# A written-out order of 1170 words replaced by another: cross-attention on one core, two softmax sums per query

## The chip, the cores and the metric

The kernel runs on one core of one Trainium2 chip. The metric is the time of the program on the device in microseconds (us); less is better. The time given is the median of three runs, and beside it stands one profiled execution, from which every row below comes.

## The reference

Two batches of 2048 tokens with 640 channels attend to 154 context rows with 1024 channels. The first 77 rows are text, the last 77 are an image prompt. There are 20 heads of 32 channels. Each head has two softmaxes, one over the text keys and one over the image keys, and their outputs are added. All is in float32.

```python
q = _split_heads(hidden_states @ Wq.T, H)
k = _split_heads(text @ Wk.T, H)
v = _split_heads(text @ Wv.T, H)
out_text = _merge_heads(_attend(q, k, v, sm_scale))
k_ip = _split_heads(ip @ Wk_ip.T, H)
v_ip = _split_heads(ip @ Wv_ip.T, H)
out_ip = _merge_heads(_attend(q, k_ip, v_ip, sm_scale))
out = (out_text + IP_SCALE * out_ip) @ Wo.T + bo
return out + residual
```

## The kernel before

The work is cut into 20 units. A unit `u` is 1024 tokens by 128 channels (four heads); two units that share batch and channels form the pair `q = u // 2`, and units 0 to 9 are batch 0. A unit has three groups `s` of 3, 3 and 2 tiles of 128 tokens. The scores of a group take four PSUM banks, one for each head, either banks 0 to 3 or banks 4 to 7.

The program is a list of 1170 words, `SCHEDULE`, and `emit` writes out the instructions of one word after another. No loop orders the work: each engine runs its instructions in the order in which the words stand, and waits where an input or a bank is not ready. A planner made the list with prices for instructions and transfers. The words are these; `R1.19@0` is group 1 of unit 19 in banks 0 to 3:

- TensorE (PE): `q` queries of a unit's half; `k`, `v` keys and values; `R` the scores (line L351); `A.q` the weighted sum over the values for a pair (L462), which needs all six groups of the pair transposed; `m`, `n`, `o`, `p`, `F` the output and query products in fast matrix schemes, which take sums of weights and of tokens as operands; `F` are the output products of batch 1, at the end of the list.
- ScalarE (ACT): `K` copies scores from PSUM to the tile `pb` (L363); `E` is the exponential; `CA`, `cq` empty banks.
- VectorE (DVE): `M` the row maxima, `D` the row sums, `I` their reciprocals, `T` the 32x32 transpose (L453), `cm`, `co`, `Y` additions into the output, and those sums of weights, `V....d`, and of tokens, `X....d`, that end in d.
- GpSimd (POOL): `S` subtracts the maxima (L425), `N` multiplies by the reciprocals (L446), and the sums `V....p`, `X....p`, `G`, `t`, `W`.
- SyncE (SP): all transfers but three, in the order of the list.

For a group the chain is R, K, M, S, E, D, I, N, T. Four sets name groups that go another way:

- `DIRECT`: no K and no S. M reads the PSUM banks (L402, four instructions), and E is 24 (or 16) small ScalarE instructions that read the banks with the maximum as bias (L387). The banks are held until E is done.
- `BIASED`: K stays, S goes; E is 24 (or 16) small ones out of `pb`.
- `SUMMED`: of these, E also accumulates the row sums, and D goes.
- `SHIFTED`: no K; VectorE subtracts out of PSUM (L415), and E is one instruction.

Of the kernel before, what the change touches and what calls it, by code (L numbers as in the profile page):

```python
# [9 lines left out]
F32 = mybir.dt.float32  # L10
# [10 lines left out]
def kernel(  # L21
# [43 lines left out]
        (1, 1), (2, 0), (2, 2), (4, 1), (6, 1), (13, 0), (13, 2), (15, 2), (16, 0), (19, 0), (19, 1), (19, 2),  # L65
    }
    BIASED = {
        (1, 2), (3, 2), (4, 2), (5, 2), (6, 2), (7, 0), (8, 0), (9, 2), (10, 0), (10, 2), (11, 2), (12, 0),
        (12, 2), (14, 1), (16, 2), (17, 1), (18, 0),
    }  # L70
    SUMMED = {
        (1, 2), (2, 0), (4, 2), (6, 1), (11, 2), (12, 0), (13, 0), (14, 1), (15, 2), (16, 0), (16, 2), (18, 0),
# [3 lines left out]
        (7, 1), (8, 1), (11, 0), (17, 0),  # L76
# [135 lines left out]
    PLACES = "012340134201342013420130414204102343123404330213"  # L212
    q_places = iter(PLACES)

# [441 lines left out]
    for _ in range(9):  # L656
# [256 lines left out]
    for c, stages in enumerate(chains_of):  # L913
        for _, text in stages:
            for _, t in terms(text):
                for h in range(NH):
                    o = int(t[0]), NH * int(t[1]) + h
# [127 lines left out]
```

## Time and profile before

| | |
|---|---|
| median of 3 runs | 504.8 us (504.4 to 506.38) |
| the profiled execution | 505.93 us, its span 504.1 us |
| mean granted TensorE clock | 0.993 |
| busy: PE, DVE, ACT, POOL | 493.4, 429.0, 335.6, 352.3 us |
| SBUF and DRAM traffic by DMA | 71.51 MB, mean 142 GB/s |

A busy time is the sum of an engine's instructions in the trace. Float32 matmuls show as two records each. A row of the timeline gives the start, the length, the engine, the line and the operation, with "xN" for N instructions merged into one row, and in brackets the idle time of the engine before it and what ended it. The attentions `A.0` to `A.9` started at 68.4, 107.8, 147.06, 184.5, 219.9, 265.8, 309.1, 350.4, 388.34 and 430.9 us, and they serve below as milestones.

### The profile page before, as it was taken

How to read it: one execution, taken by the hardware profiler on the slowest of the kernel's cores; microseconds unless marked ns; L12 is line 12 of the kernel's file. 1: busy time of each engine (PE TensorE's matmuls, PEld its weight loads, DVE VectorE, ACT ScalarE, POOL GpSimd, SP SyncE). 2: the span in 40 equal slices, each digit the busy share in tenths (PEclk: the TensorE clock that was granted, in tenths of full speed). 3: DMA queues.
4: the chain of work that ended last, by engine and by line, in shares of the span. 5: the costliest groups of instructions: out<-in, count | busy, mean ns of one | idle time of the engine just before them, and what ended most of it. 6: DMA issues, size and time to landing. Idle time of an engine off the chain costs nothing.

```text
span 504.1 us, 11093 instructions
## 1 busy us (share of the span) xinstructions
PE 493.4 (98%) x4248; PEld 321.2 (64%) x4248; DVE 429.0 (85%) x473; ACT 335.6 (67%) x1218; POOL 352.3 (70%) x172
## 2 busy tenths in 40 slices
PE   9999999999999999999999999999999989999996
PEld 5756756847645867868687676866755656444443
DVE  0089878997979999999999897999798997898877
ACT  1379988878897786888996987689679584100000
POOL 0087857766877989999898387897448938375730
PEclk9999999999999999999999999999999979999999
DMA  8992260271352526766763654266812001420115
GB/s 294 352 306 67 58 163 2 76 188 32 90 134 100 189 79 200 264 232 207 242 220 111 200 174 148 67 203 217 275 48 84 22 2 62 148 83 1 42 72 220
DMA packets 64996, 71.51 MB, mean 142 GB/s; under 512 B 5552, under 2 KB 46896, under 8 KB 63920
## 3 DMA queue, kind: packets, MB, share of 16 engines
q1 hardware_dynamic: 64256, 70.16, 44.1%
q8 instruction: 33, 0.54, 0.4%
q10 hardware_dynamic: 688, 0.66, 0.4%
q14 instruction: 19, 0.16, 0.1%
HBM read 50.74 MB, written 16.78 MB: 134 GB/s over the span
## 4 chain that ended last, share of the span: by engine, by line
PE 84%; DVE 5%; DMA 4%; ACT 3%; POOL 2%; issue 1%; SPq 1%; DVEq 0%; POOLq 0%
PE bank L218 18%; PE bank L998 11%; PE bank L351 10%; PE bank L462 9%; PE bank L148 9%; PE bank L620 9%; PE bank L302 8%; PE bank L601 5%; ACT pb L387 3%; PE bank L630 2%; PE bank L311 2%; DMA x<-in_x_dram 2%; DVE den L436 1%; DVE pb L977 1%; DMA x<-td 1%
## 5 line engine op out<-in xcount | busy, mean ns | idle before, releaser
L446 POOL TENSOR_TENSOR pb<-pb,rden 128x1848 f32<-128x1848 f32 (+1 forms) x60 | 175.9, 2944 | 51.2 <-DVE rden L441 43.7
L425 POOL TENSOR_TENSOR pb<-pb,mx 128x1848 f32<-128x1848 f32 (+1 forms) x27 | 82.5, 3057 | 52.9 <-DVE mx L399 52.7
L453 DVE STREAM_TRANSPOSE pb<-pb 128x1920 f32<-128x1920 f32 (+1 forms) x60 | 115.1, 1932 | 1.3 <-POOL pb L446 1.0
L399 DVE TENSOR_REDUCE mx<-pb 128x24 f32<-128x1848 f32 (+1 forms) x44 | 80.2, 1824 | 31.5 <-ACT pb L363 31.5
L387 ACT ACTIVATE pb<-pb,mx 128x77 f32<-128x77 f32 x328 | 96.0, 374 | 0.5 <-DVE mx L399 0.3
L436 DVE TENSOR_REDUCE den<-pb 128x24 f32<-128x1848 f32 (+1 forms) x46 | 85.3, 1855 | 9.7 <-ACT pb L387 4.8
L218 PE MATMUL bank<-x,wq_pair 128*128 128x512 f32 x200 | 89.4, 598 | 0.0
L363 ACT COPY pb<-bank 128x462 f32<-128x462 f32 (+1 forms) x176 | 74.3, 531 | 17.0 <-PE bank L351 14.7
L387 ACT ACTIVATE pb<-bank,mx 128x77 f32<-128x77 f32 x256 | 69.7, 398 | 14.9 <-DVE mx L402 14.9
L351 PEld LDWEIGHTS bank<-kT,qT 32*128 32x128 f32 x1280 | 50.7, 186 | 24.4 <-issue 8.5
L351 PE MATMUL bank<-kT,qT 32*128 32x154 f32 x1280 | 62.5, 309 | 3.6 <-ACT pb L387 3.3
L218 PEld LDWEIGHTS bank<-x,wq_pair 128*128 128x128 f32 x200 | 37.7, 192 | 43.4 <-issue 42.7
L462 PE MATMUL bank<-pb,v 32*32 32x512 f32 x1600 | 56.8, 597 | 0.8 <-issue 0.8
L431 ACT ACTIVATE pb<-pb 128x1848 f32<-128x1848 f32 (+1 forms) x31 | 52.1, 1685 | 5.8 <-POOL pb L425 5.7
L148 PE MATMUL bank<-wo_ct,aT 128*128 128x154 f32 x320 | 45.8, 296 | 0.0
L148 PEld LDWEIGHTS bank<-wo_ct,aT 128*128 128x128 f32 x320 | 43.2, 188 | 4.1 <-issue 3.4
L462 PEld LDWEIGHTS bank<-pb,v 32*32 32x32 f32 x1600 | 30.7, 103 | 22.8 <-issue 11.8
L387 ACT ACTIVATION_READ_ACCUMULATOR pb<-bank,mx 128x1 f32 x152 | 40.8, 278 | 0.0
L601 PE MATMUL bank<-aT,wo_ct 128*128 128x512 f32 x80 | 36.3, 596 | 0.0
L402 DVE TENSOR_REDUCE mx<-bank 128x6 f32<-128x462 f32 (+1 forms) x64 | 33.5, 585 | 2.7 <-PE bank L351 2.7
L620 PE MATMUL bank<-aT,wo_ct 128*128 128x256 f32 x128 | 32.0, 384 | 0.0
L387 ACT ACTIVATION_READ_ACCUMULATOR pb<-pb,mx 128x1 f32 x136 | 29.6, 219 | 0.0
(109 smaller groups left out, 657.1 us busy)
## 6 DMA issues: line engine op xcount, KB each, us to landing
x<-in_x_dram SPq DMA_DIRECT2D x12, 1280.0 KB, 7.5
out_dram<-acc SPq DMA_DIRECT2D x19, 256.0 KB, 2.4
acc<-in_x_dram SPq DMA_DIRECT2D x16, 256.0 KB, 3.7
td<-x SPq DMA_DIRECT2D x4, 1024.0 KB, 5.6
x<-td SPq DMA_DIRECT2D x4, 1024.0 KB, 5.6
out_dram<-x SPq DMA_DIRECT2D x15, 256.0 KB, 2.0
v<-vS SPq DMA_DIRECT2D x160, 20.0 KB, 2.1
aT<-in_L_xattn_Wk_ip_dram SPq DMA_DIRECT2D x5, 512.0 KB, 5.2
```

The source lines that it names most:

```text
L148: nc.tensor.matmul(keys_in(out), loaded[n][:, k, :], cT[:, k, :, t, :], start=(k == 0), stop=(k == NCC - 1))
L218: nc.tensor.matmul(pq, wqs[q % 3][:, k, :], xs[place_of(u, h)][:, k, :], start=(k == 0), stop=(k == NC - 1),)
L351: nc.tensor.matmul(ps[g][:, ts(t, 2 * L)], qTs[(u, h)][g * D : (g + 1) * D, ts(st, P)], kT[g * D : (g + 1) * D, c, b].rearrange("p t l -> ...
L363: nc.scalar.copy(keys_of(u, s)[:, :, g], ps[g][:, : n * 2 * L].rearrange("p (n l) -> p n l", n=n))
L387: nc.scalar.activation(row, row if ps is None else rows_in(ps[g], n)[:, t, x], AF.Exp, bias=maxs[(u, s)][:, *one], accum_out=None if den i ...
L399: nc.vector.tensor_reduce(mx, rows_of(u, s), AX.X, ALU.max, negate=negate)
L425: nc.gpsimd.tensor_tensor(rows_of(u, s), rows_of(u, s), maxs[(u, s)].unsqueeze(3).to_broadcast([P, n, 2, L]), ALU.subtract)
L436: nc.vector.tensor_reduce(den_of(u, s), rows_of(u, s), AX.X, ALU.add)
L446: nc.gpsimd.tensor_tensor(rows_of(u, s), rows_of(u, s), rdens[(u, s)].unsqueeze(3).to_broadcast([P, n, 2, L]), ALU.mult)
L453: nc.vector.transpose(p, p)
L462: nc.tensor.matmul(pa[r][g * D : (g + 1) * D, :], v4s[q % 2][rows, g, k, :], zones[rows, :, g, k, :], start=(k == 0), stop=(k == NK - 1),)
L620: nc.tensor.matmul(part, w_of[m][:, kp, op], t_of(m, b, i)[:, kp], start=(op == kp == 0 and m in (1, 2, 5)), stop=(op == 1 and kp == 1 and ...
```

## The change

The list is another one of 1168 words. It holds the same matmuls, the same sums of weights and tokens on the same engines, and the same transfers; what changes is the order, the banks, the buffers of the query tiles (`PLACES`), and the way of eleven groups. Written (unit, group):

| group | before | after |
|---|---|---|
| (0,2) | plain | BIASED |
| (3,1) | plain | DIRECT |
| (6,1) | DIRECT, SUMMED | plain |
| (6,2) | BIASED | plain |
| (7,0) | BIASED | plain |
| (7,2) | plain | BIASED, SUMMED |
| (8,2) | plain | BIASED |
| (9,2) | BIASED | DIRECT |
| (17,0) | SHIFTED | plain |
| (17,1) | BIASED | plain |
| (18,0) | BIASED, SUMMED | plain |
| (18,1) | plain | DIRECT |
| (18,2) | plain | BIASED |

Besides, (10,2) and (12,2) accumulate their sums in E now and (12,0) no longer does. The diff, with two lines of the list:

```diff
     DIRECT = {
-        (1, 1), (2, 0), (2, 2), (4, 1), (6, 1), (13, 0), (13, 2), (15, 2), (16, 0), (19, 0), (19, 1), (19, 2),
+        (1, 1), (2, 0), (2, 2), (3, 1), (4, 1), (9, 2), (13, 0), (13, 2), (15, 2), (16, 0), (18, 1), (19, 0),
+        (19, 1), (19, 2),
     }
     BIASED = {
-        (1, 2), (3, 2), (4, 2), (5, 2), (6, 2), (7, 0), (8, 0), (9, 2), (10, 0), (10, 2), (11, 2), (12, 0),
-        (12, 2), (14, 1), (16, 2), (17, 1), (18, 0),
+        (0, 2), (1, 2), (3, 2), (4, 2), (5, 2), (7, 2), (8, 0), (8, 2), (10, 0), (10, 2), (11, 2), (12, 0),
+        (12, 2), (14, 1), (16, 2), (18, 2),
     }
     SUMMED = {
-        (1, 2), (2, 0), (4, 2), (6, 1), (11, 2), (12, 0), (13, 0), (14, 1), (15, 2), (16, 0), (16, 2), (18, 0),
+        (1, 2), (2, 0), (4, 2), (7, 2), (10, 2), (11, 2), (12, 2), (13, 0), (14, 1), (15, 2), (16, 0), (16, 2),
         (19, 0), (19, 2),
     }
     SHIFTED = {
-        (7, 1), (8, 1), (11, 0), (17, 0),
+        (7, 1), (8, 1), (11, 0),
     }
...
-    PLACES = "012340134201342013420130414204102343123404330213"
+    PLACES = "012340134201432014312032404121024314214303402140"
...
-        "V.D.0.d V.P.1.d V.Q.0.d N1.18 E2.18 CA.8 V.I.0.p X.B.p@2 V.K.0.p V.X.0.p SS.3.4 V.E.0.d R1.19@0 M1.19 E1.19 m5.3@4 "
+        "V.E.0.d SS.3.4 CA.8 I0.18 V.H.0.d I2.18 N2.18 V.T.0.d R1.19@0 m2.3@4 M1.19 cm2.3 V.I.0.p T1.18 m1.3@6 cm1.3 "
```

The first place that matters is VectorE between the row sums of unit 18 and the maxima of group (19,1). In these rows `den_18_1` is written by D1.18 and `rden_18_1` by I1.18; L977 and L975 that write `pb_91` from `wo_ct_98` or `pb_91` are the sums of weights `V`; `mx_19_1` are the maxima M1.19. Before:

```order
L436 TENSOR_REDUCE den_18_1_3722<-pb_91 128x24
L441 RECIPROCAL rden_18_1_3724<-den_18_1_3722 128x24
L977 TENSOR_TENSOR pb_91<-wo_ct_98 128x128 x2
L977 TENSOR_TENSOR pb_91<-pb_91,wo_ct_98 128x128
L975 SCALAR_TENSOR_TENSOR pb_91<-pb_91,wo_ct_98 128x128
L977 TENSOR_TENSOR pb_91<-wo_ct_98 128x128
L402 TENSOR_REDUCE mx_19_1_3841<-bank_0_69 128x3x2
```

And in the changed kernel, from D2.18 on:

```order
L437 TENSOR_REDUCE den_18_2_3806<-pb_91 128x16
L977 TENSOR_TENSOR pb_91<-wo_ct_98 128x128 x2
L977 TENSOR_TENSOR pb_91<-pb_91,wo_ct_98 128x128
L975 SCALAR_TENSOR_TENSOR pb_91<-pb_91,wo_ct_98 128x128
L977 TENSOR_TENSOR pb_91<-wo_ct_98 128x128
L442 RECIPROCAL rden_18_0_3818<-den_18_0_3804 128x24
L977 TENSOR_TENSOR pb_91<-wo_ct_98,pb_91 128x128
L442 RECIPROCAL rden_18_2_3821<-den_18_2_3806 128x16
L977 TENSOR_TENSOR pb_91<-pb_91,wo_ct_98 128x128
L403 TENSOR_REDUCE mx_19_1_3843<-bank_0_69 128x3x2
```

Before, the five sums came behind the reciprocal I1.18, which sets GpSimd going on N1.18; now seven sums come behind D2.18, with two reciprocals among them, and D0.18 and D2.18 stand ahead of them.

The second place is GpSimd between the attentions A.7 and A.8, where `mx` rows (L425, L426 after) are the subtractions S and `rden` rows (L446, L447 after) the multiplications N of the unit and group in the name. Before:

```order
L425 TENSOR_TENSOR pb_91<-pb_91,mx_17_2_3563 128x8x154
L446 TENSOR_TENSOR pb_91<-pb_91,rden_17_1_3600 128x12x154
L446 TENSOR_TENSOR pb_91<-pb_91,rden_17_2_3606 128x8x154
L446 TENSOR_TENSOR pb_91<-pb_91,rden_17_0_3610 128x12x154
L425 TENSOR_TENSOR pb_91<-pb_91,mx_18_1_3678 128x12x154
```

In the changed kernel:

```order
L426 TENSOR_TENSOR pb_91<-pb_91,mx_17_1_3520 128x12x154
L426 TENSOR_TENSOR pb_91<-pb_91,mx_17_2_3556 128x8x154
L426 TENSOR_TENSOR pb_91<-pb_91,mx_17_0_3581 128x12x154
L447 TENSOR_TENSOR pb_91<-pb_91,rden_17_1_3596 128x12x154
L426 TENSOR_TENSOR pb_91<-pb_91,mx_18_0_3599 128x12x154
L447 TENSOR_TENSOR pb_91<-pb_91,rden_17_2_3603 128x8x154
L447 TENSOR_TENSOR pb_91<-pb_91,rden_17_0_3618 128x12x154
```

Three large subtractions, S1.17, S0.17 and S0.18, have come in ahead of N0.17, the last multiplication that A.8 waits for; S1.18 and S2.18 are gone.

The third place is GpSimd between A.1 and A.2. Before:

```order
L446 TENSOR_TENSOR pb_91<-pb_91,rden_5_1_1155 128x12x154
L425 TENSOR_TENSOR pb_91<-pb_91,mx_6_0_1253 128x12x154
L446 TENSOR_TENSOR pb_91<-pb_91,rden_6_1_1282 128x12x154
L446 TENSOR_TENSOR pb_91<-pb_91,rden_6_0_1317 128x12x154
L446 TENSOR_TENSOR pb_91<-pb_91,rden_6_2_1332 128x8x154
```

In the changed kernel:

```order
L447 TENSOR_TENSOR pb_91<-pb_91,rden_5_1_1192 128x12x154
L426 TENSOR_TENSOR pb_91<-pb_91,mx_6_2_1272 128x8x154
L426 TENSOR_TENSOR pb_91<-pb_91,mx_6_1_1290 128x12x154
L426 TENSOR_TENSOR pb_91<-pb_91,mx_6_0_1294 128x12x154
L447 TENSOR_TENSOR pb_91<-pb_91,rden_6_1_1311 128x12x154
L447 TENSOR_TENSOR pb_91<-pb_91,rden_6_2_1320 128x8x154
L447 TENSOR_TENSOR pb_91<-pb_91,rden_6_0_1337 128x12x154
```

The two subtractions S2.6 and S1.6 are new there. On TensorE, the queries q.7.0, which stood ahead of A.2, follow it now.

144 rows, old and new, of the table SCHEDULE are left out of this document.

## The prediction

> **What bounds the kernel now.** I read the page first: TensorE is busy almost always, at the full clock but for one slice, and the chain that ended last runs over it for 84%.
>
> ```profile
> PE 493.4 (98%) x4248; PEld 321.2 (64%) x4248; DVE 429.0 (85%) x473; ACT 335.6 (67%) x1218; POOL 352.3 (70%) x172
> ...
> PEclk9999999999999999999999999999999979999999
> ...
> PE 84%; DVE 5%; DMA 4%; ACT 3%; POOL 2%; issue 1%; SPq 1%; DVEq 0%; POOLq 0%
> ```
>
> The matmuls are the same before and after. So the time can change only by TensorE's waits and by its clock, and the one low slice of the clock, the 33rd (from 403 us), is the first place to look. I then took the busy time by windows, four from one attention to the next and the first and the last slice; behind the window's length stand the busy times of PE, of its weight loads, of DVE, ACT and POOL, then the clock.
>
> ```profile
> 0.00:12.60 12.60, 11.55 (x34) 7.34 (x35) 0.17 (x1) 1.28 (x1) 0.83 (x6) 1.00 0.85 294
> ...
> 107.80:147.10 39.30, 38.52 (x401) 24.26 (x409) 33.83 (x31) 32.08 (x113) 28.30 (x9) 1.00 0.41 107
> 147.10:184.50 37.40, 37.02 (x398) 25.22 (x400) 35.50 (x36) 28.59 (x88) 30.52 (x20) 1.00 0.31 102
> 350.40:388.30 37.90, 37.90 (x368) 22.23 (x368) 34.60 (x36) 30.26 (x113) 23.23 (x11) 1.00 0.44 142
> 388.30:430.90 42.60, 39.30 (x322) 26.16 (x322) 36.85 (x47) 25.05 (x125) 32.23 (x23) 0.92 0.08 26
> ...
> 491.40:504.00 12.60, 8.85 (x23) 3.91 (x21) 9.02 (x16) 0.00 (x0) 0.00 (x0) 1.00 0.61 224
> ```
>
> The last stretch, A.8 to A.9, is the one with a low clock, and TensorE idles 42.60 - 39.30 = 3.3 us in it. The timeline of that stretch gives the reason.
>
> ```profile
> 393.82 1.07 PE L351 MATMUL bank<-kT,qT 32*128 32x154 f32 x24
> ...
> 394.47 0.42 DVE L977 TENSOR_TENSOR pb<-wo_ct 128x128 f32<-128x128 f32 x2
> ...
> 394.70 3.34 POOL L446 TENSOR_TENSOR pb<-pb,rden 128x1848 f32<-128x1848 f32 x1 [0.24 <-DVE pb L977]
> 394.81 3.38 DVE L977 TENSOR_TENSOR pb<-pb,wo_ct 128x128 f32<-128x128 f32 x1
> 394.82 1.13 PE L620 MATMUL bank<-x 128*128 128x256 f32 x4
> ...
> 398.46 2.40 POOL L983 TENSOR_TENSOR aT<-aT 128x1024 f32<-128x1024 f32 x1
> ...
> 398.57 2.44 DVE L977 TENSOR_TENSOR pb<-wo_ct 128x128 f32<-128x128 f32 x1
> ...
> 400.10 1.89 PE L620 MATMUL bank<-aT,wo_ct 128*128 128x256 f32 x8
> ...
> 400.93 2.26 DVE L402 TENSOR_REDUCE mx<-bank 128x6 f32<-128x462 f32 x4
> 401.59 5.28 ACT L387 ACTIVATE pb<-bank,mx 128x77 f32<-128x77 f32 x24 [5.98 <-DVE mx L402]
> ...
> 406.92 1.90 PE L351 MATMUL bank<-kT,qT 32*128 32x154 f32 x18 [0.67 <-ACT pb L387]
> ...
> 408.75 2.08 PE L620 MATMUL bank<-aT,x 128*128 128x256 f32 x4
> ...
> 413.41 3.60 PE L601 MATMUL bank<-aT,wo_ct 128*128 128x512 f32 x8
> ```
>
> R1.19 was done at 394.8, but M1.19 (L402) began only at 400.93. Ahead of it VectorE had five sums of weights. Two took 0.42 us together, one 3.38 us and one 2.44 us: each of the long ones began while a GpSimd instruction ran (394.70 to 398.04; 398.46 to 400.86) and ended with it. VectorE spent 6.5 us, from 394.47, on what is about 1.3 us of work. E1.19 (L387, direct out of the banks) came late by as much, and R0.19, which needs those banks, could not begin when m1.3 ended at 401.8 (the 24 records of m5.3 and m2.3 took 400.10 - 394.82, so 0.22 us each, and m1.3 has 8). Then the clock fell as well:
>
> ```profile
> 406.00:408.00 2.00, 1.33 (x18) 1.08 (x17) 1.84 (x3) 0.87 (x5) 0.05 (x1) 0.50 0.00 0
> ...
> 412.00:414.00 2.00, 2.00 (x8) 1.50 (x7) 2.00 (x3) 2.00 (x15) 0.28 (x1) 0.81 0.02 4
> ```
>
> Without wait and with the full clock, R0.19 (1.0 us, as R1.19 from 393.82 to 394.82) and m3.3 (12 records, 2.6 us) would have ended at 405.4; p.1 (L601) began at 413.41. **This place costs 8.0 us**: 5.1 until the last 18 records of R0.19 start at 406.92, and 2.9 by the halved clock.
>
> **The change part by part.** *Startup.* The first loads and partial queries change places. In both lists the same 14 partial queries stand ahead of the first keys, and the loads ahead of those keys are the same set; I take 0, between -1 and +1.
>
> *The place above.* I count from the end of R1.18 and follow the new list with these rows:
>
> ```profile
> 358.55 1.07 PE L351 MATMUL bank<-kT,qT 32*128 32x154 f32 x24
> ...
> 362.19 2.07 DVE L399 TENSOR_REDUCE mx<-pb 128x24 f32<-128x1848 f32 x1
> ...
> 364.29 6.09 ACT L387 ACTIVATE pb<-pb,mx 128x77 f32<-128x77 f32 x24
> ...
> 366.48 2.25 POOL L425 TENSOR_TENSOR pb<-pb,mx 128x1232 f32<-128x1232 f32 x1 [7.98 <-DVE mx L399]
> ...
> 374.18 1.38 DVE L436 TENSOR_REDUCE den<-pb 128x16 f32<-128x1232 f32 x1
> ...
> 378.03 2.12 DVE L453 STREAM_TRANSPOSE pb<-pb 128x1920 f32<-128x1920 f32 x1
> ...
> 379.56 4.56 PE L601 MATMUL bank<-aT,wo_ct 128*128 128x512 f32 x10
> ...
> 388.34 5.55 PE L462 MATMUL bank<-pb,v 32*32 32x512 f32 x160
> ...
> 390.38 1.73 ACT L431 ACTIVATE pb<-pb 128x1848 f32<-128x1848 f32 x1
> ...
> 409.11 0.33 ACT L387 ACTIVATE pb<-bank,mx 128x77 f32<-128x77 f32 x1 [2.24 <-DVE mx L402]
> ...
> 416.22 0.34 ACT L387 ACTIVATION_READ_ACCUMULATOR pb<-bank,mx 128x1 f32 x1
> ```
>
> TensorE: q.19.0 and o.3 took 8.8 us (379.56 to 388.34), A.8 5.5 (to 393.82), R1.19 1.0, and m2.3, m1.3, m5.3 7.0 (394.82 to 401.83). R0.19 is due at 22.3. ScalarE: let M1.18 start d after R1.18 ends. E1.18, now direct, starts 0.66 later (401.59 - 400.93) and takes 5.3; E0.18, now one instruction, 1.7; E2.18, now 16 small ones at 6.09 / 24, 4.1. They end at 11.8 + d. VectorE: D2.18 1.4; then seven sums at about 0.25 and two reciprocals of about 0.3, 2.3 in all, if GpSimd lets them. It does: N1.18 is released by D1.18, which follows E1.18, and with 3.3 us it ends near 12 + d, before the sums begin at 13.2 + d; the next, N2.18, waits for the reciprocal among them. The last sum, V.T, stands right behind that reciprocal; the row at 394.70 shows that VectorE's next sums started first there and GpSimd waited 0.24. So M1.19 starts at 15.5 + d, E1.19 ends at 21.5 + d, and R0.19 waits for d - 0.8 if that is above nothing.
>
> d comes from GpSimd. M1.18 stands behind T1.17 (2.1), which needs N1.17, and S1.17, S2.17 and S0.17 stand ahead of N1.17 now: 3.3 + 2.25 + 3.3 + 3.3 = 12.2 us from the end of M1.17. In the trace M1.17 ended at 364.26, 5.7 after R1.17 began, and GpSimd had then been idle (7.98 us before 366.48), so this work starts at once: N1.17 ends at 17.9 and T1.17 at 20.1 after R1.17's start. Between that start and R1.18's end TensorE has 21.0 (358.55 to 379.56; the same words stand there in both lists). d is 0 if nothing else is late; since VectorE must fit its other reductions of unit 17 in between I take 1.5, with ends 0 and 4. Then N0.17 ends 8.9 us after N1.17 (S0.18, N2.17, N0.17), T0.17 at some 29, and A.8 is due at 21.0 + 8.8 = 29.8: that holds by less than 1 us, a wait there is likely if d is above 1, and it delays R0.19 too, so that of the two waits only the longer counts. I take 1.5 for both, between 0 and 5.
>
> E0.19 follows: from 409.11 to 416.56, with 0.68 from its maxima's start, 8.1 us against m6.3, m3.3 and p.1 with 7.8 us on TensorE. Before, the slow clock covered that; now R2.19 waits about 0.4. A.9 then needs T2.19. Behind R2.19 TensorE has 11.2 us (m7.3 1.7, p.0 and p.3 3.4 each by the row at 413.41, m4.3 2.6), against some 10 for M2.19, E2.19 (16 / 24 of 7.45), N2.19 and T2.19: it holds with 1 us to spare, and I add 0.6 for it.
>
> Before, some 4 us passed between the start of the wait (401.8) and the fall of the clock (near 406). No wait of that size remains by this count, so of the 8.0 us there remain 1.5 + 0.4 + 0.6 = 2.5, and **5.5 us are gained**, between 0 and 8.
>
> [...]
>
> *A.1 to A.3.* GpSimd gets S2.6 and S1.6, 5.6 us, while q.7.0 (4.3 us) leaves the stretch A.1 to A.2: 28.30 + 5.6 = 33.9 us of work in 39.3 - 4.3 = 35.0 us. Only what A.2 needs must be done in it, and that ends with N1.5, which both lists have ahead of the new subtractions; the surplus goes into the next stretch, which is 4.3 us longer and gets some 2 us more work (30.52 in 37.40 before). I take 0, between -0.5 (A.2's banks are emptied behind q.7.0 now) and +6.
>
> *The rest* (the other groups, earlier and later transfers of x): ScalarE loses some 4 us of work and GpSimd gains some 3, both off the path. TensorE idles 504.1 - 493.4 = 10.7 us in all, 3.3 of it at the place above and 1.05 and 3.75 in the first and the last slice, so other waits are worth 2.6 at most; a new order may make as many anew. I take +0.3, between -2 and +3.
>
> **Sum.** 505.93 (the profiled execution, span 504.1 and 1.8 around it) - 5.5 + 0.3 = 500.7. It stood 1.1 above the median of the runs, so for the median: 504.8 - 5.2 = **499.6 us**. A measurement of this kernel can tell about 0.5%, 2.5 us, from no change.
>
> **The rivals.**
> *The wait stays.* If GpSimd's longer queue makes d 4 us, R0.19 waits 3.2, and 4.2 of the 8.0 remain (with the 0.4 and 0.6): 504.8 - 3.8 + 0.3 = 501.3. If the clock falls again, 2.9 more: 504.2. If besides N2.18 takes its turn ahead of V.T (2.25): 506.5. For it: three large subtractions came in on that queue; against it: 23.23 of 37.90 us were busy there. I put the time at 504.2; chance 0.20.
> *GpSimd becomes the bound between A.1 and A.3.* It had 11.0 us idle of 39.3 there, mostly waiting for inputs; of 35.0 us only 1.1 are left now. If half of the old idle time stays, each of its results is 4.4 us late at A.3, TensorE waits that long, the clock costs 2.9 more, and the next attention pays some of it again: + 8 to + 12. It decides from a lateness of some 5 us; 504.8 - 5.2 + 9 = 508.6, slower than before. Against it: from 147.1 to 184.5 VectorE ran at 95% and GpSimd at 82%, and TensorE idled 0.38 us. Chance 0.16.
> *Nothing remains.* d is 0, all of the 8.0 goes and some small waits too: 504.8 - 9 = 495.8. Chance 0.14.
>
> **How the numbers follow.** My own case has 0.50, with a range of its own from 497.5 to 502. Faster by over 0.5% are my case and the last rival, 0.64; the same is the first, 0.20; slower the second, 0.16. The range leaves out the worst of the slower cases and a little below: 495.0 to 507.0.
>
> **What would show it.** In the profile after: no slice with a low PEclk; the sums of L977 between D2.18 and M1.19 at 0.2 to 0.4 us each; A.8 to A.9 at some 36 us instead of 42.6; a short wait of TensorE on VectorE's transpose before A.8. The prediction is wrong if TensorE idles over 3 us at another attention or at R0.19, or if the stretch A.1 to A.3 grows beyond its 76.7 us.

## The result and the profile after

| | before | after |
|---|---|---|
| median, six runs of each side by side | 505.08 us | 497.52 us |
| ratio, 95% interval | | 0.9855, 0.9835 to 0.9875 |
| profiled execution, its span | 505.93, 504.1 us | 496.94, 495.2 us |
| mean granted clock | 0.993 | 1.0 |

The changed kernel is 1.45% faster, 7.6 us. It lies 2.1 us below the predicted 499.6, inside the range, at the lower edge of the range given for the likeliest case. (In the experiments below the ratios leave out one execution of 1745.11 us, out of twelve with TensorE kept busy.) The page of the profile after shows TensorE's busy time 4.9 us shorter for the same matmuls, no slice of low clock, and a last chain that is TensorE alone:

```profile
PE 488.5 (99%) x4248; PEld 317.8 (64%) x4248; DVE 422.8 (85%) x472; ACT 330.8 (67%) x1189; POOL 355.0 (72%) x172
...
PEclk9999999999999999999999999999999999999999
...
PE 98%; DMA 1%; issue 0%; ACT 0%; DVE 0%; ACTq 0%; DVEq 0%
```

The busy time by windows from one attention to the next (columns as in the prediction, then the DMA share and GB/s), for A.1 to A.3 and for A.8 to A.9:

```profile
107.40:142.30 34.90, 34.14 (x383) 22.61 (x382) 31.58 (x26) 23.34 (x58) 27.07 (x10) 1.00 0.55 139
142.30:183.70 41.40, 41.02 (x402) 26.76 (x401) 39.06 (x38) 34.28 (x102) 37.34 (x22) 1.00 0.32 102
386.80:421.90 35.10, 35.10 (x321) 23.74 (x320) 32.23 (x48) 23.73 (x124) 29.22 (x21) 1.00 0.10 32
```

The last stretch took 42.55 us before (388.34 to 430.89) and takes 35.07 now (386.84 to 421.91), and TensorE has no wait left in it: 35.10 us busy in a window of 35.10. That is 7.5 of the 9.0 us by which the end of TensorE's work moved (500.25 to 491.27). The timeline of this place after:

```profile
376.31 1.81 PE L352 MATMUL bank<-kT,qT 32*128 32x154 f32 x40
376.73 2.12 DVE L454 STREAM_TRANSPOSE pb<-pb 128x1920 f32<-128x1920 f32 x1
378.77 2.24 DVE L403 TENSOR_REDUCE mx<-bank 128x6 f32<-128x462 f32 x4
...
383.68 2.13 DVE L454 STREAM_TRANSPOSE pb<-pb 128x1920 f32<-128x1920 f32 x1
...
386.84 5.55 PE L463 MATMUL bank<-pb,v 32*32 32x512 f32 x160
...
388.26 3.29 POOL L447 TENSOR_TENSOR pb<-pb,rden 128x1848 f32<-128x1848 f32 x1 [1.71 <-DVE rden L442]
...
388.60 3.41 DVE L437 TENSOR_REDUCE den<-pb 128x24 f32<-128x1848 f32 x2
...
391.93 0.28 DVE L977 TENSOR_TENSOR pb<-wo_ct 128x128 f32<-128x128 f32 x1
392.43 0.29 DVE L977 TENSOR_TENSOR pb<-wo_ct 128x128 f32<-128x128 f32 x1 [0.22 <-PE bank L463]
...
393.88 0.23 DVE L977 TENSOR_TENSOR pb<-pb,wo_ct 128x128 f32<-128x128 f32 x1
394.03 2.26 DVE L403 TENSOR_REDUCE mx<-bank 128x6 f32<-128x462 f32 x4
394.11 2.25 POOL L447 TENSOR_TENSOR pb<-pb,rden 128x1232 f32<-128x1232 f32 x1 [2.56 <-DVE pb L977]
...
400.42 1.07 PE L352 MATMUL bank<-kT,qT 32*128 32x154 f32 x24
...
405.83 3.60 PE L602 MATMUL bank<-aT,wo_ct 128*128 128x512 f32 x8
...
409.36 1.24 PE L352 MATMUL bank<-kT,qT 32*128 32x154 f32 x16
```

GpSimd is idle from 391.55 to 394.11, and the five sums and the two behind them lie in just that gap: each takes 0.23 to 0.29 us, where one took 3.38 and one 2.44 before. So M1.19 starts at 394.03, 7.2 us behind the start of A.8 instead of 12.6, and R0.19 starts at 400.42 with no wait ahead of it. The long sums of before ended with the GpSimd instruction that ran beside them: GpSimd 394.70 to 398.04, the sum 394.81 to 398.19; GpSimd 398.46 to 400.86, the sum 398.57 to 401.01. What holds such a sum up is not shown. Other VectorE work beside GpSimd was not held up: the two row sums at 388.60, which read one tile each, ran beside N1.18 and took 3.41 us, no more than the 2.04 and 1.38 us that such sums take elsewhere.

The other 1.5 us: A.0 starts 0.55 earlier (67.79 for 68.34), and from A.0 to A.8 it takes 319.05 us for 320.00. TensorE had waited for transfers, 0.45 us up to 295.0 and 0.39 us up to 308.1; both waits are gone. From the start of A.9 to TensorE's end it is 69.36 us in both.

### The profile page after: what moved, and what is told of

Same layout as the page of the kernel before. It is cut to its first block, busy times and chain, and to the rows that moved or that the text cites. A ratio compares the mean times of both kernels' runs of the same rounds, so it can differ in the third digit from the quotient of the medians.

```text
span 495.2 us, 11084 instructions
## 1 busy us (share of the span) xinstructions
PE 488.5 (99%) x4248; PEld 317.8 (64%) x4248; DVE 422.8 (85%) x472; ACT 330.8 (67%) x1189; POOL 355.0 (72%) x172
## 4 chain that ended last, share of the span: by engine, by line
PE 98%; DMA 1%; issue 0%; ACT 0%; DVE 0%; ACTq 0%; DVEq 0%
PE bank L219 21%; PE bank L998 11%; PE bank L352 11%; PE bank L463 11%; PE bank L303 10%; PE bank L621 10%; PE bank L149 9%; PE bank L602 7%; PE bank L312 3%; PE bank L631 3%; DMA wq_pair<-in_L_xattn_Wq_dram 1%; ACT qT L232 0%; DVE acc L933 0%; ACTq L182 0%; DVEq L1040 0%
## 5 line engine op out<-in xcount | busy, mean ns | idle before, releaser
L447 POOL TENSOR_TENSOR pb<-pb,rden 128x1848 f32<-128x1848 f32 (+1 forms) x60 | 176.0, 2944 | 40.5 <-DVE rden L442 24.7
L426 POOL TENSOR_TENSOR pb<-pb,mx 128x1848 f32<-128x1848 f32 (+1 forms) x27 | 85.5, 3174 | 53.4 <-DVE mx L400 53.4
L400 DVE TENSOR_REDUCE mx<-pb 128x24 f32<-128x1848 f32 (+1 forms) x43 | 78.7, 1836 | 29.9 <-ACT pb L364 29.5
L437 DVE TENSOR_REDUCE den<-pb 128x24 f32<-128x1848 f32 (+1 forms) x46 | 87.1, 1897 | 10.5 <-ACT pb L388 7.4
L388 ACT ACTIVATE pb<-pb,mx 128x77 f32<-128x77 f32 x288 | 86.1, 398 | 0.4 <-DVE mx L400 0.4
L388 ACT ACTIVATE pb<-bank,mx 128x77 f32<-128x77 f32 x296 | 76.3, 393 | 8.6 <-DVE mx L403 8.6
L352 PEld LDWEIGHTS bank<-kT,qT 32*128 32x128 f32 x1280 | 49.0, 184 | 19.8 <-issue 9.7
L352 PE MATMUL bank<-kT,qT 32*128 32x154 f32 x1280 | 60.5, 307 | 0.6 <-ACT kT L826 0.4
L403 DVE TENSOR_REDUCE mx<-bank 128x6 f32<-128x462 f32 (+1 forms) x68 | 35.1, 577 | 5.1 <-PE bank L352 5.0
L388 ACT ACTIVATION_READ_ACCUMULATOR pb<-bank,mx 128x1 f32 x128 | 33.4, 266 | 0.0
L388 ACT ACTIVATION_READ_ACCUMULATOR pb<-pb,mx 128x1 f32 x136 | 32.4, 241 | 0.0
```

The costliest lines, as they stand in the source:

```text
L352: nc.tensor.matmul(ps[g][:, ts(t, 2 * L)], qTs[(u, h)][g * D : (g + 1) * D, ts(st, P)], kT[g * D : (g + 1) * D, c, b].rearrange("p t l -> ...
L388: nc.scalar.activation(row, row if ps is None else rows_in(ps[g], n)[:, t, x], AF.Exp, bias=maxs[(u, s)][:, *one], accum_out=None if den i ...
L400: nc.vector.tensor_reduce(mx, rows_of(u, s), AX.X, ALU.max, negate=negate)
L426: nc.gpsimd.tensor_tensor(rows_of(u, s), rows_of(u, s), maxs[(u, s)].unsqueeze(3).to_broadcast([P, n, 2, L]), ALU.subtract)
L437: nc.vector.tensor_reduce(den_of(u, s), rows_of(u, s), AX.X, ALU.add)
L447: nc.gpsimd.tensor_tensor(rows_of(u, s), rows_of(u, s), rdens[(u, s)].unsqueeze(3).to_broadcast([P, n, 2, L]), ALU.mult)
```

## The experiments

Every kernel below is one of the two lists with one edit; its line numbers are a few lower or higher. Each of three sets of runs has its own runs of before, with medians of 505.6, 505.7 and 505.29 us.

**The two lists joined at A.6.** One list up to 24 words ahead of A.6, the other from there on. A product next to the joint has a bank of its own, so that the banks fit.

> The list of before up to attention A.6, the changed list from there on. By the two traces the place A.8 to A.9 gave 7.5 us and all that lies ahead of A.8 1.5 us. Theory (the two parts add): 7.2 to 7.8 us faster than before, 497 to 498. Rival (part of the gain at the place rests on what the head of the changed list does): less than 6.5 us faster.

> The changed list up to attention A.6, the list of before from there on. Theory (the two parts add): 1.2 to 1.9 us faster than before, 503 to 504; the wait ahead of A.9 and the slices of 5 are still there. Rival (the head alone brings nothing, its 1.5 us being a shift that is lost again at the next wait): within 0.5 us of before.

> The changed kernel itself, as the control of the two mixed lists: the list of before up to A.6 with the changed list behind it was 5.3 us faster than before (500.3), the reverse 1.8 us slower (507.4). Theory (the two parts add, the head bringing 1 to 2 us): 498 to 499.5, that is 6 to 7.5 us faster than before. Rival (the head brings nothing, or costs something, and the first comparison was lucky): 500 to 502.

Measured: the changed end alone 500.34 us (ratio 0.9892, 0.9865 to 0.9919); the changed head alone 507.39 (1.0032, 1.0008 to 1.0055); both, the changed kernel again, 497.46 (0.9845, 0.9831 to 0.9859). The windows from A.8 to A.9 of these three, in this order, show what the end does:

```profile
388.44:423.51 35.07, 35.07 (x321) 23.70 (x320) 32.21 (x48) 23.70 (x123) 29.23 (x21) 1.00 0.10 32
```
```profile
391.81:434.58 42.77, 39.37 (x321) 26.29 (x321) 36.79 (x47) 25.01 (x124) 32.19 (x23) 0.92 0.08 26
```
```profile
387.87:422.94 35.07, 35.07 (x321) 23.70 (x320) 32.19 (x48) 23.70 (x123) 29.22 (x21) 1.00 0.10 32
```

By the windows the 7.5 us come with the end of the list, whatever the head. By the medians the two parts do not add as I expected: the changed end alone gained 5.3 us, which is the rival's number, and the changed head alone lost 1.8 us, which fits neither. The profile of the first is the fastest of its six executions (498.56 to 501.86 us, mean granted clock 0.995 to 1.0), and that of the second the slowest of its twelve (505.27 to 509.6 us, clock 0.99 to 0.993), so no trace shows what the others lost or gained. The profile with the changed head alone has two losses that the changed kernel's has not: a wait ahead of A.6 that I read as the joint's, and a low clock behind TensorE's stop inside A.1, from 116 us on:

```profile
306.32 1.13 PE L300 MATMUL bank<-x,x 128*128 128x256 f32 x4 [1.53 <-DVE qS L328]
...
116.00:118.00 2.00, 2.00 (x27) 1.56 (x25) 0.76 (x1) 0.70 (x3) 2.00 (x1) 0.58 0.23 52
```

By the medians the head is worth 2.9 us on top of the changed end, by the profiles about 1 (A.0 to A.8, above). What of the difference is the joint's is open.

**The sums moved, before's list.** The five sums from behind I1.18 to behind M1.19. GpSimd's sum V.I, which reads one of them, then stands ahead of it and adds other numbers.

```diff
-... A.8@1 cq.19.0 V.P.0.d V.D.0.d V.P.1.d V.Q.0.d N1.18 ... V.E.0.d R1.19@0 M1.19 E1.19 ...
+... A.8@1 cq.19.0 N1.18 ... R1.19@0 M1.19 V.P.0.d V.D.0.d V.P.1.d V.Q.0.d V.E.0.d E1.19 ...
```

> The list of before, with one edit: the five weight sums that VectorE makes next to attention A.8 (its 393-401 us) go right behind the maxima M1.19. Theory (the sums ran beside GpSimd's normalizing products, held M1.19 back and with it the scores R0.19, and the slow clock followed from that wait): M1.19 starts near 395 instead of 401 us, TensorE's row before A.9 has no slice of low clock, A.8 to A.9 takes 35 to 37 us instead of 42.6, and the time falls by 6 to 8 us to 497-499. Rival (it was the lighter work of unit 18, its groups with fewer products on GpSimd and sums on ScalarE, that removed the wait): the wait stays above 3 us and the time falls by less than 3 us.

Measured: 503.18 us, ratio 0.9955 (0.9934 to 0.9976), 2.4 us faster: the rival's number. The profile shows the theory's mechanism and a new wait that takes half of the gain back. First the timeline, then the window A.8 to A.9:

```profile
395.72 2.28 DVE L400 TENSOR_REDUCE mx<-bank 128x6 f32<-128x462 f32 x4 [0.32 <-PE bank L349]
...
399.25 2.35 POOL L979 TENSOR_TENSOR aT<-aT 128x1024 f32<-128x1024 f32 x1
399.32 2.43 DVE L973 TENSOR_TENSOR pb<-wo_ct 128x128 f32<-128x128 f32 x1 [0.35 <-POOL pb L973]
...
402.74 1.07 PE L349 MATMUL bank<-kT,qT 32*128 32x154 f32 x24
...
413.65 1.97 PE L618 MATMUL bank<-aT,x 128*128 128x256 f32 x8 [3.47 <-DVE acc L649]
```
```profile
389.18:428.16 38.98, 35.43 (x322) 23.37 (x321) 35.22 (x49) 24.96 (x124) 32.11 (x23) 1.00 0.09 28
```

M1.19 starts 6.5 us behind the start of A.8 (12.6 before), R0.19 does not wait, the clock stays whole. But a sum meets GpSimd again at 399.3, everything behind it on VectorE is late, and at 410 TensorE waits 3.5 us for a bank that VectorE empties. The place gained 3.6 us of 7.5.

**The sums left out, before's list.** The same five words are taken out, nothing is moved.

> The list of before without the five weight sums that VectorE makes next to A.8 (their work is left out, so the three sums and the products behind them work on other numbers). In the earlier run that moved them behind M1.19 the wait of R0.19 went, but the place gained 3.6 us only, since the moved sums and what stood behind them made TensorE wait 3.5 us at 410 us. Theory (the sums beside GpSimd's products are the whole of the 8 us): R0.19 starts without a wait, no low clock, A.8 to A.9 takes 34.5 to 36 us instead of 42.6, and the time falls by 6.5 to 8 us. Rival (part of the gain came from the lighter unit 18 and the new order behind it): a wait of 2 to 4 us stays between R0.19 and A.9, and the time falls by 3 to 5 us.

Measured: 499.75 us, ratio 0.9893 (0.9874 to 0.9913), 5.5 us faster, between the two. By the window the place gained 6.2 of the 7.5 us:

```profile
388.20:424.56 36.36, 35.35 (x321) 23.37 (x321) 32.71 (x44) 24.96 (x124) 32.00 (x23) 1.00 0.09 30
```
```profile
398.23 2.35 POOL L979 TENSOR_TENSOR aT<-aT 128x1024 f32<-128x1024 f32 x1
398.39 2.33 DVE L973 TENSOR_TENSOR pb<-wo_ct,pb 128x128 f32<-128x128 f32 x1
...
410.05 1.96 PE L618 MATMUL bank<-aT,x 128*128 128x256 f32 x8 [1.01 <-DVE acc L649]
```

So the five sums carry most of the cost (with the collisions, their own 1.3 us on VectorE are gone here too). Of the last 1.3 us TensorE's wait of 1.0 us for the same bank is the greater part: a sixth sum, at 398.39, still collides here. That the changed order behind the five takes this wait away is read from the profile after, and was not tried by itself.

**The sums moved back, changed list.** They go right behind I1.18 again. Standing ahead of A.8, they write over values that A.8 still reads.

```diff
-... D1.18 I1.18 o.3@1 G7.3 N1.18 co.3 A.8@1 D0.18 D2.18 V.P.0.d V.D.0.d V.P.1.d V.Q.0.d V.E.0.d ...
+... D1.18 I1.18 V.P.0.d V.D.0.d V.P.1.d V.Q.0.d V.E.0.d o.3@1 G7.3 N1.18 co.3 A.8@1 D0.18 D2.18 ...
```

> The changed list, with the same five weight sums moved ahead, right behind the reciprocal I1.18, so that they run beside GpSimd's products N1.18 again. Theory (the collision is what costs): sums that start inside N1.18 last until it ends, near 391.6 us (rows of 2 to 3 us instead of 0.2 to 0.4); M1.19 comes 1.5 to 3 us later, TensorE waits for it ahead of R0.19, and the time rises by 1.5 to 3.5 us over the changed kernel, more (up to 6) if the clock falls. Rival (where the sums stand does not matter by itself): within 0.5 us of the changed kernel.

Measured: 504.77 us, ratio to before 0.9971 (0.9945 to 0.9998). That is 7.2 us above the changed kernel, more than either theory gave.

```profile
391.19 3.34 POOL L444 TENSOR_TENSOR pb<-pb,rden 128x1848 f32<-128x1848 f32 x1 [1.71 <-DVE pb L973]
391.30 3.37 DVE L973 TENSOR_TENSOR pb<-pb,wo_ct 128x128 f32<-128x128 f32 x1
...
394.82 7.57 PE L460 MATMUL bank<-pb,v 32*32 32x512 f32 x160 [4.98 <-DVE pb L973]
```

The collision is made anew: the sum that took 0.28 us takes 3.37, beside GpSimd's 3.34. Its price is not measured by this kernel, since A.8 itself now waits for the sums, 5.0 us, and then takes 7.57 us for 5.55, which I read as a low clock. My expectation had missed that.

**TensorE kept busy, before's list.** Six matmuls (`zz.6`) ahead of R0.19, where it waited.

```diff
-... m1.3@6 I2.18 R0.19@0 ...
+... m1.3@6 I2.18 zz.6 R0.19@0 ...
+        elif k == "zz":
+            keys = kT.rearrange("p c b t l -> p (c b t l)")
+            for _ in range(x):
+                nc.tensor.matmul(banks[5], keys[:, :P], keys[:, P : P + TB], start=True, stop=True)
```

> The list of before, with six extra matmuls of 512 columns (5.15 us at full clock, results unused) on TensorE right ahead of the scores R0.19, where it waited 5.1 us. Theory (the half clock that follows the wait comes from the wait): the waits of 402-407 us shrink by what the matmuls fill, no slice of the clock is below 9, and the time falls by about the 2.9 us that the slow clock cost, to 501.5-503. Rival (the clock falls for another reason, such as the load before): the slices of 5 stay and the time is the same within 1 us, or 5 us longer if the matmuls do not fall into the wait.

Measured: 504.07 us, ratio 0.997 (0.9952 to 0.9987), 1.5 us faster with more work, if less than expected. The timeline, then a window:

```profile
400.99 5.31 PE L751 MATMUL bank<-kT 128*128 128x512 f32 x12
...
406.23 1.07 PE L349 MATMUL bank<-kT,qT 32*128 32x154 f32 x24
```
```profile
400.00:408.00 8.00, 8.00 (x46) 4.48 (x45) 7.62 (x13) 5.28 (x24) 3.05 (x5) 1.00 0.00 0
```

R0.19 starts 18.7 us behind A.8, where its last 18 records started in before too (18.6), and runs at the full clock: A.8 to A.9 took 40.17 us, 2.4 less than before. So the low clock came from the wait, and 2.4 us is its measured price, where the prediction had 2.9.

**More work on GpSimd, changed list.** Idle adds of 128x128 (`zp.7`: seven of them, 3.26 us) ahead of S0.17; fourteen, and then six, behind N1.5.

```diff
-... I1.17 S0.17 M0.18 ...
+... I1.17 zp.7 S0.17 M0.18 ...
-... LK.19 N1.5 cv.3.1 R2.6@1 ...
+... LK.19 N1.5 zp.14 cv.3.1 R2.6@1 ...      (and zp.6 in the third kernel)
```

> The changed list with 3.3 us more on GpSimd (seven idle adds of 128x128, 0.45 to 0.5 us each, results unused) ahead of the subtraction S0.17. My prediction let GpSimd's queue of unit 17 hold A.8 back by 1.5 us; the trace of the changed kernel shows no wait there, with the transpose T0.17 done 1 us ahead of A.8. Theory (the queue is that near to the path): A.8 waits 2 to 2.5 us, and the time rises by 1.5 to 2.8 us. Rival (the slack is larger, other work fills it): less than 0.8 us.

> The changed list with 6.6 us more on GpSimd (fourteen idle adds of 128x128, results unused) behind the products N1.5, between A.1 and A.3. Theory (GpSimd's 64.4 busy of 76.3 us there are no bound, its 12 us of idle time take the adds): the time rises by less than 1.5 us. Rival of the prediction (GpSimd becomes the bound between A.1 and A.3): the time rises by 4 to 6.6 us.

> The changed list with 2.8 us more on GpSimd (six idle adds, results unused) at the place where 6.6 us more had cost 5.8 us, behind N1.5. There TensorE waited 3.3 us, so that 3.3 of the 6.6 us were hidden. Theory (a slack of 3.3 us, the rest of the 5.8 us being the slow clock after the wait): no wait, within 0.7 us of the changed kernel. Rival (no slack, each us on GpSimd costs about one): 2 to 3 us slower.

Ahead of S0.17: 501.08 us, ratio to before 0.9877 (0.982 to 0.9934), some 3.6 us above the changed kernel.

```profile
389.65 7.14 PE L462 MATMUL bank<-pb,v 32*32 32x512 f32 x160 [2.15 <-DVE pb L453]
...
390.00:392.00 2.00, 2.00 (x57) 1.39 (x41) 1.97 (x3) 2.00 (x10) 0.05 (x1) 0.61 0.03 8
```

A.8 waits for the transpose T0.17, as expected and by the expected amount: 2.15 of the 3.26 us show, so about 1.1 had been to spare. What I had not counted is the clock, which fell behind a wait of that size: A.8 took 7.14 us for 5.55. It need not fall: of the four executions of this kernel one took 499.14 us with a mean granted clock of 1.0.

Behind N1.5, fourteen adds: 503.28 us, 0.9943 (0.9907 to 0.9979), 5.8 us above the changed kernel. The rival is right here.

```profile
143.89 8.74 POOL L425 TENSOR_TENSOR pb<-pb,mx 128x1232 f32<-128x1232 f32 x3
...
149.43 1.75 ACT L431 ACTIVATE pb<-pb 128x1848 f32<-128x1848 f32 x1 [13.41 <-POOL pb L425]
...
154.79 2.04 ACT L485 COPY aT<-bank 128x512 f32<-128x512 f32 x4
...
155.42 5.93 PE L351 MATMUL bank<-kT,qT 32*128 32x154 f32 x64 [3.10 <-ACT aT L485]
```

ScalarE stands at 149.43 on an exponential that needs GpSimd's subtraction, and the copies that empty the banks of A.2 are behind it in its queue; the next scores need those banks. TensorE waits 3.1 us, then runs the scores at half clock (0.50 from 157 to 161 us; 5.93 us for 3.30). GpSimd's idle time, 12 us between A.1 and A.3, was no measure of the room in front of this one instruction. Six adds: 498.41 us, 0.9879 (0.986 to 0.9898), 1.0 us above the changed kernel, between the two expectations, and no such wait. So some 3 us of work fit there without a wait, though not quite for nothing.

**The loads earlier, before's list.** The load of x BX.5 and the fetch TI.0 go ahead to behind cn4.3.0.

```diff
-... K2.12 D1.11 M1.12 TI.0 LQ.9 BX.5 E2.11 ...
+... I1.10 cn4.3.0 TI.0 BX.5 K2.11 WS.1.1 ...
```

> The list of before, with the load of x (BX.5) and the fetch of stored sums (TI.0) issued as early as in the changed list, right behind the copy cn4.3.0, 24 places ahead in the list. Theory (TensorE's wait of 0.74 us at 294 us is for that load): the wait is gone, A.6 starts 0.7 us earlier or more, and the time falls by 0.5 to 1.0 us. Rival (the queue ahead of the load, not its place, sets its start): the wait stays, the time is the same within 0.3 us.

Measured: 505.68 us, 0.9993 (0.9965 to 1.0021). The number is the rival's, but the run does not decide between the two, because the edit moved another load than the one TensorE waits for. BX.5 goes out at 237.14 us here, long ahead of A.5 (265.93). The load that lands as the wait ends is issued at 286.71; by the order of the list it is BX.7, behind the eight transfers of VS.7.1, which the edit left in place. The wait stays, 0.79 us, where before's own row has 0.45 and not the 0.74 of the expectation:

```profile
279.78 5.69 SPq L162 DMA_DIRECT2D v<-vS  x8
...
286.71 0.38 SPq L200 DMA_DIRECT2D x<-in_x_dram  x1
...
295.53 1.13 PE L300 MATMUL bank<-x,wq_pair 128*128 128x256 f32 x4 [0.79 <-DMA x<-in_x_dram]
```

In the changed list BX.7 stands ahead of VS.7.1 and goes out at 283.19 us. That this is why the changed kernel has no wait there is only argued; it was not tried by itself.

**Forty matmuls ahead of A.1, changed list** (one execution), on TensorE's stop inside A.1.

> The changed list with forty more matmuls of 32 columns (results unused) right ahead of A.1. In both kernels TensorE stops for 1.3 us inside A.1, behind its 1984th matmul, 4.9 us after A.1 starts, with no other engine that releases it. Theory (the stop hangs on the number of instructions that TensorE's queue has passed): it comes 40 matmuls, about 1.1 us, earlier within A.1, again behind the 1984th. Rival (it hangs on what A.1 reads): it stays 4.9 us after A.1 starts. The time rises by the matmuls' own 0.6 to 1.5 us.

The execution took 512.44 us, 14.9 above the changed kernel. The forty took 14.4 us, far more than expected even without the clock: at the full clock their 80 records start 0.11 us apart, which makes 8.9 us of them (an estimate from the first 27), and I put the rest down to the half clock (0.50 from 112 us on). The stop of 1.3 us went: in A.1 no two instructions of TensorE start more than 0.57 us apart. It neither moved by forty matmuls nor stayed, so both forms of my expectation fail. What A.1 reads is not excluded as the cause: A.1 read the same, but 14.6 us later and at a low clock (0.50 from 122 to 126 us; 8.13 us for 5.5).

## Why the prediction was right, and where its sizes were off

- *The place.* Right: the collision of sums with GpSimd, the late M1.19, the wait, the clock. The runs without the sums, with the sums elsewhere and with TensorE kept busy show each link. The mis-sized term is the residue: "5.5 gained, 2.5 remain". 7.5 were gained and nothing remained; the 8.0 was itself counted 0.5 too large. For the profiled execution the sum gave 500.7 and 496.94 came: of the 3.8 between them the place is 2.0, the startup 0.55, and the rest, A.1 to A.3 among it, 1.25.
- *d, "I take 1.5".* M1.18 starts 378.77 - 378.12 = 0.65 behind the end of R1.18, since VectorE begins T1.17 at 376.73, while R1.18 still runs. With 0.65 the prediction's own rule, "R0.19 waits for d - 0.8", gives no wait. Nor did A.8 wait for T0.17, done at 385.81, 1.0 ahead of it; the short wait there, named as a sign, did not come. The margin "by less than 1 us" was right, and the run with 3.26 us more on GpSimd shows that it is a real one.
- *R2.19 0.4, A.9 0.6.* Neither came: R2.19 starts right at the end of p.1 (409.43), and the window to A.9 has no wait. I had added three small waits to a place where each had a margin near zero; that all three fell on the side of none was luck as much as reckoning.
- *Startup 0.* -0.55 in the profile, inside its bounds, and not the list's: the profiles of before's head run from 67.75 to 68.34, of the changed head from 67.78 to 69.27.
- *A.1 to A.3, 0.* 76.25 us for 76.63. Right, but for a weak reason, so with luck: I compared sums of work and idle time over 35 us. The margin sits at one subtraction and is about 3 us; the rival's point of decision, "a lateness of some 5 us", was put too high, and its price too: 5.8 measured, with the clock, for 8 to 12.
- *The rest, +0.3.* -1.0 from A.0 to A.8, the 0.4 of A.1 to A.3 among it. Two waits for transfers, 0.8 together, went, and I had set them against new ones that did not come.
- *The rivals.* "The wait stays" and "GpSimd becomes the bound" did not occur. "Nothing remains" (495.8) describes the place better than my own case, and its time is the nearer one too (1.7 off for 2.1); it overshot by its 9 us.
- *The clock behind a wait.* The 2.5 us that were to remain have no low clock in them. That a wait of 1.5 us brings none was my estimate from one place, where some 4 us passed between the start of the wait and the fall of the clock. Here a wait of 2.15 us ahead of A.8 was enough (0.61 in the rows behind it), though not in every execution. What a wait of 1.5 us does to the clock no run shows: had A.8 waited so long, the clock need not have stayed.

## What to carry to other kernels

Look at which instructions of two engines run side by side, not only at how busy each engine is: a sum that takes 0.28 us elsewhere started 0.11 us inside GpSimd's 3.34 us instruction and took 3.38 us here, and the maxima behind it in the list began at 400.93, 6 us after their scores were done. The cure here was a place in the list where the other engine waited anyway (GpSimd, 391.55 to 394.11). The room on an engine is read at the one instruction that a waiting queue needs next (12 us of idle time on GpSimd, about 3 us of room), and a wait of TensorE should be priced with the low clock behind it (2.4 us here).

## What was not expected of the hardware

The clock fell without any idle time of TensorE that the profile shows. Ahead of A.1 the forty matmuls with 32 columns kept it and its weight loads busy throughout from 107.7 us, and some three us later, near 110.6, the granted clock went down:

```profile
107.70:110.00 2.30, 2.30 (x23) 2.30 (x21) 2.16 (x4) 2.09 (x3) 1.15 (x2) 1.00 1.18 316
110.00:112.00 2.00, 2.00 (x14) 2.00 (x13) 2.00 (x3) 0.00 (x0) 2.00 (x1) 0.67 1.18 289
112.00:114.00 2.00, 2.00 (x11) 2.00 (x11) 1.97 (x3) 0.00 (x0) 0.92 (x2) 0.50 1.20 298
```

So in this one execution instructions that ran without a break did not hold the clock. What does hold it was not tested.

And TensorE stops inside A.1 in every kernel but the last: 4.9 us after A.1 starts, and behind the same instruction of its stream in all of them (about the 1985th, with weight loads and semaphore instructions), 0.6 to 1.9 us pass until the next one starts, with no other engine that releases it. The clock fell behind it in two of these thirteen profiles (0.50 from 117 to 119 us), with stops of 1.5 and 1.9 us, and not in others with 1.5 and 1.8.

The cause was not shown by an edit, but the traces point to a transfer. The page counts 33 packets and 0.54 MB on a DMA queue that it names "instruction" (q8), 16 KB each. In all thirteen profiles one such packet starts 3.0 to 4.2 us behind the start of A.1, and TensorE goes on 2.5 to 2.8 us behind the start of that packet, so the later the packet, the longer the stop:

| kernel | packet starts, behind A.1 | TensorE goes on, behind the packet's start | stop |
|---|---|---|---|
| sums moved, before's list | 3.0 us | 2.5 us | 0.6 us |
| before | 3.6 | 2.7 | 1.4 |
| after | 3.6 | 2.7 | 1.3 |
| sums moved back, changed list | 4.0 | 2.8 | 1.9 |

With the forty matmuls the packet came 9.8 us ahead of A.1, and there was no stop, though A.1 ran at a low clock there too (8.13 us, 0.50). What these packets bring, and to which engine, is not shown; if the one behind A.1 is the cause, its price is the stop of 0.6 to 1.9 us.
